# Two attention layers on a 4096-node graph: other sums, accumulators and order in the last microseconds of layer two

## The chip, the cores and the metric

The kernel runs on one core of a Trainium2 chip. The metric is the device time of one execution in microseconds (us); of several runs the median is given. PE is TensorE (matmuls), DVE is VectorE, ACT is ScalarE, POOL is GpSimd, SP is SyncE, which here only issues transfers (DMAs). Line numbers (L1731) are those of the kernel before.

## The reference

The inputs are 4096 rows of 512 features `x`, a sparse 0/1 adjacency matrix `adj`, and the weights of two graph attention layers, all float32. Layer one is a four-headed additive attention with a residual and a layer norm. Layer two, in which the change lies, is masked dot-product attention of eight heads of width 64, then a residual and a layer norm:

```python
adj = jnp.maximum(adjacency_matrix, eye)
q = jnp.einsum('nd,hdk->hnk', node_matrix, Wqs)
k = jnp.einsum('nd,hdk->hnk', node_matrix, Wks)
v = jnp.einsum('nd,hdk->hnk', node_matrix, Wvs)
scores = jnp.einsum('hqk,hmk->hqm', q, k) * kd ** (-0.5)
scores = scores + IDENTITY_BIAS * eye - MASK_VAL * (1.0 - adj)
att = jax.nn.softmax(scores, axis=-1)
return jnp.einsum('hqm,hmk,hko->qo', att, v, Wo)
...
x = _layernorm(x + _L1_gnn_ref(x, adj, L1_gnn_Wks, L1_gnn_Wqs, L1_gnn_Wvs, L1_gnn_Wo), axis=-1)
```

## The kernel before

All engines run their instructions in the order in which the code issues them; there is no scheduler behind it. Layer two works on pairs `(g, m)`: `g` is one of 8 groups of 512 query rows, `m` one of 4 pairs of heads. A pair has 32 units `j`, one for each 128 key rows. For a unit PE computes the scores of two heads into a PSUM tile `s_ps` (128 x 1024, three buffers), ACT takes the exponential in place (L1551), and VectorE multiplies by the mask into a weight tile `p` (L1554). One step later PE multiplies the weights into the output `o_ps` (L1599). A step takes three units; the last pair has its step of two units in the middle (`n_short`), so its last step is of three.

The softmax needs the sum of a pair's weights. `add_up` makes it from the tiles `p`, two at a time: a transfer with addition puts the second of two on the first (L1584, issued from POOL), and POOL adds the result to `q_sum` (L1574). `Later` delays both: `later.at(n, f)` runs `f` at the n-th next `later.step()`, and each step ends in one. POOL also multiplies a pair's output by the reciprocal sums (`on`, L1637), and four small instructions of each layer norm are POOL's (`normal_factors`, L514 to L519).

The last 10 of the last pair's weight tiles are not summed that way: `last_sum` collects them. VectorE adds the first six into one (L1731), and the column sums on PE (`all_sums`, L1605) take six accumulators: `q_sum`, that sum, and the last four tiles themselves.

The output rows are worked in tiles of 128. `project` multiplies a tile of `on` by the output weights, four head pairs `m` accumulating in PSUM (L1663). `close1` adds layer one's row (loaded by `load_y`) on VectorE (L1673), takes the statistics there (L510, L512), the factors on POOL, and one step or more later ACT normalises (L1678) and SP stores. Most tiles are projected and closed while later pairs run. Five are left for the end: tile -5 (of group 6), and the four of group 7, which need the last pair. Behind the last step the code runs: the last products; the VectorE adds; projection and closing of tile -5; the first three quarters of two projections; the column sums; `divide_at_once` (four times a reciprocal, L1655, and a product, L1656, each 128 rows, then two ACT sums, L1659); then, tile by tile, the remaining quarters and the closings, with a test of ranges (`all_in_range`) whose result, `counted` (L1754), decides whether a general path runs instead.

Of the kernel before, what the change touches and what calls it, by code (L numbers as in the profile page):

```python
# [8 lines left out]
F32 = mybir.dt.float32  # L9
# [3 lines left out]
AF = mybir.ActivationFunctionType  # L13
ALU = mybir.AluOpType
# [4 lines left out]
P = 128  # L19
EPS = 1e-5  # L20
# [6 lines left out]
F_MAX = 40.0  # L27
SUM_MIN = 1e-20
SUM_MAX = 1e30
# [400 lines left out]
def tile_gat_then_masked_attention(  # L430
# [16 lines left out]
    nc = tc.nc  # L447
    N, D = x.shape
    H0, D0, _ = weight_u.shape
    H1, _, KD = wks.shape  # L450
    NT = N // P
    G = 512
    NG = N // G
    GT = G // P
    KC = D // P
    HP = P // KD
    NP1 = H1 // HP
# [19 lines left out]
    small = main.enter_context(tc.tile_pool(name="small", bufs=6))  # L477
# [4 lines left out]
    minus_half = const.tile([P, 1], F32, name="minus_half")  # L482
# [36 lines left out]
        nc.gpsimd.tensor_scalar(nb, nb, -1.0, None, op0=ALU.mult)  # L519
        return rs, nb  # L520

    def all_in_range():

        ok = small.tile([P, 8], F32, name="ok")
        ends = small.tile([P, 6], F32, name="ends")
        for n, op in ((0, ALU.max), (2, ALU.min)):
            nc.vector.tensor_reduce(ends[:, 2 + n:4 + n],
                                    span[:, :, n:n + 2].rearrange("p g k -> p k g"), AX.X, op)
        nc.vector.tensor_reduce(ends[:, 0:1], total, AX.X, ALU.add)
        nc.vector.tensor_reduce(ends[:, 1:2], most, AX.X, ALU.add)  # L530
        for n, (value, limit, op) in enumerate((
                (ends[:, 2:3], F_MAX, ALU.is_le), (ends[:, 3:4], F_MAX, ALU.is_le),
                (ends[:, 4:5], -F_MAX, ALU.is_ge), (ends[:, 5:6], -F_MAX, ALU.is_ge),
                (ends[:, 0:1], SUM_MAX, ALU.is_le), (ends[:, 1:2], 1.0 / SUM_MIN, ALU.is_le))):
            nc.vector.tensor_scalar(ok[:, n:n + 1], value, limit, None, op0=op)
        all_ok = small.tile([P, 1], F32, name="all_ok")
        nc.vector.tensor_reduce(all_ok, ok[:, 0:6], AX.X, ALU.min)
        return all_ok
# [6 lines left out]
    counted = const.tile([1, 1], I32, name="counted")  # L545
    right = main.enter_context(ExitStack())
    xp = right.enter_context(tc.tile_pool(name="xp", bufs=2, space=PSUM, side="right"))
    later = Later()
# [18 lines left out]
    with tc.tile_pool(name="l0", bufs=NG) as l0, \  # L567
# [77 lines left out]
        with tc.tile_pool(name="l0s", bufs=2) as sp:  # L645
# [175 lines left out]
            tiles, base = {}, {}  # L821
# [88 lines left out]
            for g in range(NG):  # L910
# [7 lines left out]
                for k, (kind, i) in enumerate(plan):  # L918
                    if k in (0, 3, 7, 10):
                        t = (0, 3, 7, 10).index(k)  # L920
# [63 lines left out]
        with wait_by_tile("l0v", 2) as vp:  # L984
# [91 lines left out]
            for n, (w, h, j) in enumerate(steps):  # L1076
# [7 lines left out]
                p = p_t.pop((w, h, j))  # L1084
                s = sup[w * H0 + h, j // GT][:, j % GT, :]
# [11 lines left out]
    with wait_by_tile("l1", 1) as l1, wait_by_tile("l1a", 2) as lp, \  # L1097
# [417 lines left out]
        with wait_by_tile("l1w", 2) as wp, wait_by_tile("l1o", 1, space=PSUM) as op:  # L1515
# [42 lines left out]
            def add_up(g, m, j):  # L1558

                if j % 2 == 0:
                    return
                a, b = pt.pop((g, m, j - 1)), pt.pop((g, m, j))
                i, n = j // 2, NT // 2
                at_end = (g, m) == pairs[-1]

                def first():
                    q_sum[g, m] = wp.tile([P, HP, G], F32, name="q_sum")
                    nc.gpsimd.tensor_tensor(q_sum[g, m], a, b, op=ALU.add)  # L1570

                def add(p):
                    q = q_sum[g, m]
                    nc.gpsimd.tensor_tensor(q, q, p, op=ALU.add)  # L1574

                if i == 0:
                    later.at(1, first)
                elif at_end and i >= n - 5:
                    last_sum.extend((a, b))
                elif i % 8 == 7:  # L1580
                    later.at(2, lambda: add(a))
                    later.at(3, lambda: add(b))
                else:
                    later.at(2, lambda: nc.gpsimd.dma_start(a, b, accum_op=ALU.add))  # L1584
                    later.at(5, lambda: add(a))

            last_sum = []

            def products(g, m, j):
                if j == 0:  # L1590
# [11 lines left out]
            def all_sums(qs, s):  # L1602
                for n, q in enumerate(qs):
                    for c in range(0, P, MA):
                        nc.tensor.matmul(s[c:c + MA, :], ones[:, 0:MA], q[:, c // KD, :],  # L1605
                                         start=(n == 0), stop=(n == len(qs) - 1))
# [51 lines left out]
                    den = wp.tile([P, G], F32, name="den1", bufs=1)  # L1658
                    nc.scalar.activation(den, src, AF.Copy, accum_out=sums[:, n:n + 1])  # L1659

            def project(g, t, s, ms=range(NP1)):
                for m in ms:
                    nc.tensor.matmul(s, on_t[g][:, m, t * P:(t + 1) * P], wo_sb[:, m, :],  # L1663
                                     start=(m == 0), stop=(m == NP1 - 1))

            def load_y(g, t):
                y_t[g, t] = wp.tile([P, D], F32, name="y1", bufs=5)
                nc.sync.dma_start(y_t[g, t], x1_d[g][t * P:(t + 1) * P, :])

            def close1(g, t, s, wait=4):  # L1670
                i = g * GT + t
                y = y_t.pop((g, t))
                nc.vector.tensor_tensor(y, y, s, op=ALU.add)  # L1673

                rs, nb = normal_factors(y)

                def normalise():
                    nc.scalar.activation(y, y, AF.Identity, bias=nb, scale=rs)  # L1678
                    nc.sync.dma_start(out[i * P:(i + 1) * P, :], y)
                later.at(wait, normalise)  # L1680

            per_pair = [list(range(j, min(j + NB, NT))) for j in range(0, NT, NB)]
            n_short = 5
# [5 lines left out]
            def step(batch, extra_sum, extra_tile, wait=4):  # L1691
                got = [scores(*u) for u in batch]
                if extra_tile and extra_tile not in y_t:
                    load_y(*extra_tile)
                if extra_sum or extra_tile:
                    extra = ps.tile([P, HP, G], F32, name="s_ps")
                if extra_sum:
                    half_sums(q_sum.pop(extra_sum), extra[:, 0, :])
                if extra_tile:
                    project(*extra_tile, extra[:, 1, :])  # L1700
                for u, su in zip(batch, got):
                    weigh(*u, su)
                if extra_tile:
                    close1(*extra_tile, extra[:, 1, :], wait)
                if extra_sum:
                    divide(*extra_sum, extra[:, 0, :])
                for u in batch:
                    add_up(*u)
                for g, m, j in last:
                    products(g, m, j)  # L1710
                for g, m, j in last:
                    if j == NT - 1:
                        o_sb[g, m] = wp.tile([P, G], F32, name="o_sb")
                        o = o_t.pop((g, m))
                        nc.scalar.activation(o_sb[g, m], o[:, 0, :], AF.Copy)
                        nc.vector.tensor_tensor(o_sb[g, m], o_sb[g, m], o[:, 1, :], op=ALU.add)
                last[:] = batch
                later.step()

            for n, (g, m) in enumerate(pairs):  # L1720
                for js in per_pair if n + 1 < len(pairs) else last_pair:
                    whole = len(js) == NB
                    step([(g, m, j) for j in js],
                         None if whole or n < 1 else pairs[n - 1],
                         None if whole or n < NP1 + 1 else tiles[n - NP1 - 1])
            for t in tiles[-5:]:
                load_y(*t)
            step([], None, None)
            later.step()
            for p in last_sum[1:-4]:  # L1730
                nc.vector.tensor_tensor(last_sum[0], last_sum[0], p, op=ALU.add)  # L1731
            step([], None, tiles[-5], 2)
            y_ps = ps.tile([P, HP, G], F32, name="s_ps")
            den_ps = ps.tile([P, HP, G], F32, name="s_ps")
            o_ps = op.tile([P, 2, G], F32, name="o1_ps")
            y_ps = [y_ps[:, 0, :], y_ps[:, 1, :], o_ps[:, 0, :], o_ps[:, 1, :]]
            for n in range(2):
                project(*tiles[n - GT], y_ps[n], range(NP1 - 1))
            all_sums([q_sum.pop(pairs[-1]), last_sum[0]] + last_sum[-4:], den_ps[:, 0, :])
            divide_at_once(*pairs[-1], den_ps[:, 0, :])  # L1740
            for n in range(GT):
                if n + 2 < GT:
                    project(*tiles[n + 2 - GT], y_ps[n + 2], range(NP1 - 1))
                project(*tiles[n - GT], y_ps[n], [NP1 - 1])
                if n == GT - 2:
                    continue
                if n == GT - 1:
                    all_ok = all_in_range()
                    close1(*tiles[n - 1 - GT], y_ps[n - 1], 1)
                close1(*tiles[n - GT], y_ps[n], 1)  # L1750
                later.step()
            count = den_ps[0:1, 1, 0:1]
            nc.tensor.matmul(count, all_ok, ones[:, 0:1], start=True, stop=True)
            nc.vector.tensor_copy(counted, count)  # L1754
            later.flush()


# [34 lines left out]
```

## Time and profile before

| What | Value |
|---|---|
| Median of 4 runs | 3326.25 us (3323.81 to 3326.94) |
| The profiled execution | 3325.09 us, span 3323.2 us |
| PE busy | 3299.7 us (99%) |
| POOL, DVE, ACT busy | 2173.5, 2478.1, 1948.7 us |
| PE's share of the chain that ended last | 92% |
| Last products of layer two | 3283.2 to 3286.0 us |
| VectorE adds of the last weights (L1731) | 3287.36 to 3296.74 us |
| Column sums behind them (L1605) | 3296.78 to 3301.28 us |
| First reciprocal (L1655) | 3301.42 us |
| Last normalised row tile (L1678) | 3315.56 to 3316.37 us |

Times within the span are counted from its start. Busy time is the sum of an engine's instructions; an engine that is busy all the time may still not set the end of a stretch. The chain that ended last is followed back from the last instruction, at each step to what released it. The landing time of a transfer is counted from the start of its issue.

### The profile page before, as it was taken

Reading aid. Unit: us, or ns where it says so; the run is one execution under the profiler, and the core shown is the slowest. Engines: PE = TensorE matmul, PEld = TensorE weight load, DVE = VectorE, ACT = ScalarE, POOL = GpSimd, SP = SyncE. Lnnn points to the kernel's source line nnn. Section 1 sums busy time; section 2 is a strip of 40 time slices with the busy share of each in tenths; the row PEclk is TensorE's granted clock in tenths of the full one; section 3 lists DMA queues with packets and bytes.
Section 4 is the critical chain, followed back from the end, with each engine's and each line's share of the span. In section 5 each row is a group of like instructions: output and inputs, shape, how many; then the busy total and the mean of one; then the engine's idle time right before and its main releaser. Section 6 shows DMA issues by size and latency. Waiting matters only on the chain.

```text
span 3323.2 us, 67217 instructions
## 1 busy us (share of the span) xinstructions
PE 3299.7 (99%) x27160; PEld 1964.4 (59%) x27160; DVE 2478.1 (75%) x3186; ACT 1948.7 (59%) x2439; POOL 2173.5 (65%) x1602
## 2 busy tenths in 40 slices
PE   9999999999999999999999999999999999999998
PEld 8899999999999777733333333333333333333333
DVE  6689899899999677467667666676666766667666
ACT  1367868878776310156656566566665656656564
POOL 5630040040030244389999999999999999999996
PEclk9999999999999999999999999999999999999999
DMA  8989796686532443489898988879888899897984
GB/s 185 228 201 184 219 186 168 151 183 147 137 93 58 110 149 116 167 214 208 190 211 223 227 196 197 209 188 260 199 197 209 188 219 239 194 211 185 213 195 112
DMA packets 398993, 612.06 MB, mean 184 GB/s; under 512 B 167632, under 2 KB 248528, under 8 KB 398672
## 3 DMA queue, kind: packets, MB, share of 16 engines
q0 software_dynamic: 97520, 258.77, 42.7%
q1 hardware_dynamic: 299280, 345.88, 33.6%
q8 instruction: 216, 3.54, 0.4%
q10 hardware_dynamic: 1872, 3.02, 0.4%
q14 instruction: 105, 0.86, 0.1%
HBM read 315.87 MB, written 109.25 MB: 128 GB/s over the span
## 4 chain that ended last, share of the span: by engine, by line
PE 92%; POOL 3%; DMA 2%; DVE 1%; issue 1%; ACT 0%; POOLq 0%; SPq 0%; DVEq 0%; ACTq 0%
PE o_ps L1087 27%; PE o_ps L1599 24%; PE s_ps L1138 24%; PE o_ps L846 4%; PE s_ps L1663 3%; PE s_ps L1298 2%; PE s_ps L1248 2%; PE s_ps L1255 2%; DMA p<-p 2%; POOL q_sum L1574 2%; PE x_ps L1255 1%; PE x_ps L1248 1%; POOL p L1584 1%; PE s_ps L1618 0%; DMA y_sb<-in_x_dram 0%
## 5 line engine op out<-in xcount | busy, mean ns | idle before, releaser
L1574 POOL TENSOR_TENSOR q_sum<-q_sum,p 128x1024 f32<-128x1024 f32 x538 | 1375.2, 2556 | 66.4 <-DMA p<-p 44.0
L1554 DVE TENSOR_TENSOR p<-s_ps,adjT 128x1024 f32<-128x1024 f32 x896 | 1044.3, 1216 | 469.2 <-ACT s_ps L1551 435.3
L1551 ACT ACTIVATE s_ps<-s_ps 128x1024 f32<-128x1024 f32 x1021 | 967.6, 1006 | 597.0 <-PE s_ps L1138 596.6
L1138 PE MATMUL s_ps<-q_sb,k_sb 64*64 64x512 f32 x8192 | 943.9, 589 | 2.1 <-DVE p L1554 2.0
L1599 PE MATMUL o_ps<-p,v_sb 64*64 64x512 f32 x8192 | 943.6, 590 | 0.0
L1087 PE MATMUL o_ps<-sup_t,p 128*128 128x129 f32 x8192 | 915.7, 275 | 1.2 <-DVE p L640 1.2
L1087 PEld LDWEIGHTS o_ps<-sup_t,p 128*128 128x128 f32 x8192 | 915.3, 192 | 1.7 <-DVE p L640 1.4
L640 DVE SCALAR_TENSOR_TENSOR p<-fr_t,dj,az 128x1024 f32<-128x1024 f32 x512 | 650.2, 1284 | 66.1 <-PE o_ps L1087 37.9
L1138 PEld LDWEIGHTS s_ps<-q_sb,k_sb 64*64 64x64 f32 x8192 | 312.1, 133 | 569.9 <-issue 451.5
L1599 PEld LDWEIGHTS o_ps<-p,v_sb 64*64 64x64 f32 x8192 | 310.2, 133 | 570.6 <-issue 560.4
L624 ACT ACTIVATE z<-fr_t,f 128x1024 fp8e4<-128x1024 f32 x512 | 557.3, 1143 | 102.0 <-DVE az L635 101.7
L1584 POOL DMA_DIRECT2D p<-p x412 | 439.0, 1305 | 10.1 <-PE o_ps L1599 9.2
L1063 POOL DMA_DIRECT2D agg<-base_d x32 | 29.1, 1217 | 386.8 <-DMA sup_t<-sup_d 204.7
L585 POOL COPY seen<-token 128x1 f32<-128x1 f32 x24 | 10.9, 455 | 356.8 <-DVE token L583 356.8
L1554 DVE TENSOR_TENSOR p<-s_ps,md 128x1024 f32<-128x1024 f32 x128 | 150.8, 1218 | 66.8 <-ACT s_ps L1551 59.6
L635 DVE TENSOR_TENSOR az<-adjT,z 128x512 int32<-128x512 int32 x256 | 175.3, 685 | 2.9 <-ACT z L624 1.7
L600 ACT ACTIVATE adjT<-stage 128x1024 fp8e4<-128x1024 bf16 x128 | 130.9, 1051 | 16.6 <-DMA stage<-adj_d 16.6
L1663 PE MATMUL s_ps<-wo_sb,on 128*128 128x512 f32 x240 | 110.8, 604 | 0.0
L1633 ACT ACTIVATE r<-r_h 32x256 f32<-32x256 f32 x248 | 102.3, 412 | 2.9
L1049 ACT ACTIVATE agg<-o_ps,rinv 128x128 f32<-128x128 f32 x128 | 42.1, 370 | 70.5 <-DVE den L1042 46.8
L1322 ACT ACTIVATE v<-s_ps 128x256 f32<-128x256 f32 x28 | 10.7, 383 | 115.0 <-PE s_ps L1298 99.9
L1663 PEld LDWEIGHTS s_ps<-wo_sb,on 128*128 128x128 f32 x240 | 43.3, 189 | 55.9 <-issue 55.7
(275 smaller groups left out, 2231.6 us busy)
## 6 DMA issues: line engine op xcount, KB each, us to landing
p<-p POOLq DMA_DIRECT2D x412, 512.0 KB, 9.1
k_sb<-k_d SPq DMA_DIRECT2D x128, 512.0 KB
v_sb<-v_d SPq DMA_DIRECT2D x128, 512.0 KB
adj_d<-in_adj_dram POOLq DMA_DIRECT2D x32, 1024.0 KB, 11.1
sup_t<-sup_d SPq DMA_DIRECT2D x120, 258.0 KB
fr_t<-fr_d SPq DMA_DIRECT2D x16, 1024.0 KB
adjT_d<-adjT SPq DMA_DIRECT2D x32, 512.0 KB
adjT<-adjT_d SPq DMA_DIRECT2D x32, 512.0 KB
```

Of the source, the lines that this page charges most:

```text
L624: nc.scalar.activation(z[:, k, :], fr_t[w, h][:, 0, :], AF.Sign, bias=fs[j // GT][:, 0, (j + k) % GT, h:h + 1], saturate=False)
L635: nc.vector.tensor_tensor(az.bitcast(I32), adjT[w, j // CJ][:, j % CJ:j % CJ + 2, :].bitcast(I32), z.bitcast(I32), op=ALU.bitwise_and)
L640: nc.vector.scalar_tensor_tensor(p, fr[:, 1, :], dj[j // GT][:, j % GT, h:h + 1], az_t[w, h, j // 2][:, j % 2, :], op0=ALU.max, op1=ALU.mult)
L846: nc.tensor.matmul(out[:, t * HD:(t + 1) * HD], xb[:, c, t * P:(t + 1) * P], wb[:, c, :], start=not more and t == 0 and c == 0, stop=c == ...
L1087: nc.tensor.matmul(o[t // BK][:, t % BK, :], p[:, t * P:(t + 1) * P], s, start=(j == 0 and t % BK == 0), stop=(j == NT - 1), skip_group_ch ...
L1138: nc.tensor.matmul(s[c:c + MS, e, :], k[r, a + c:a + c + MS], qt[g, m][r, :], start=True, stop=True)
L1551: nc.scalar.activation(s, s, AF.Exp, scale=float(KD) ** -0.5)
L1554: nc.vector.tensor_tensor(p, s, keep[:, None, :].to_broadcast([P, HP, G]), op=ALU.mult)
L1574: nc.gpsimd.tensor_tensor(q, q, p, op=ALU.add)
L1584: later.at(2, lambda: nc.gpsimd.dma_start(a, b, accum_op=ALU.add))
L1599: nc.tensor.matmul(o[c, n, :], v[r, j % CH, c], p[r, e, :], start=(j == 0), stop=(j == NT - 1))
L1663: nc.tensor.matmul(s, on_t[g][:, m, t * P:(t + 1) * P], wo_sb[:, m, :], start=(m == 0), stop=(m == NP1 - 1))
```

## The change

The change touches the end of layer two alone, in six places.

1. In `add_up`, weights 22 to 27 of the last pair are now added in twos by transfers, and only one tile of each two is kept; weights 28 to 31 are kept as before. `last_sum` is 22, 24, 26, 28, 29, 30, 31.
2. VectorE adds all seven into tile 22, in two parts (`gather`): 24, 28 and 29 ahead of the addition of the last pair's two output halves, then 30, 31 and 26. The column sums take two accumulators: `q_sum` and tile 22.
3. Tile -5 is projected ahead of the last products instead of behind them; its closing comes behind all of VectorE's adds.
4. ACT copies layer one's rows into the four PSUM accumulators of the last four tiles, and the projections add onto them (`onto`); the rows are loaded earlier in the program.
5. The partial projections and the last products are issued as part 0, part 1, column sums, part 2, rest 0, rest 1, part 3, rest 2, rest 3, and the closings behind all of them.
6. The closings (`close_in_place`) take statistics and normalisation from PSUM. Three are normalised by ACT as before; the last one on VectorE, with two small POOL instructions instead of four. The range test is split: what doesn't need the sums comes ahead of the column sums.

```diff
                 elif at_end and i >= n - 5:
-                    last_sum.extend((a, b))
+                    later.at(2, lambda: nc.gpsimd.dma_start(a, b, accum_op=ALU.add))
+                    last_sum.append(a)
...
-            def project(g, t, s, ms=range(NP1)):
+            def project(g, t, s, ms=range(NP1), onto=False):
                 for m in ms:
                     nc.tensor.matmul(s, on_t[g][:, m, t * P:(t + 1) * P], wo_sb[:, m, :],
-                                     start=(m == 0), stop=(m == NP1 - 1))
+                                     start=(m == 0 and not onto), stop=(m == NP1 - 1),
+                                     skip_group_check=onto)
...
+            def close_in_place(g, t, s, vector=False, meanwhile=None):
+                i = g * GT + t
+                y = y_t.pop((g, t))
+                st = small.tile([P, 6], F32, name="bn_st")
+                nc.vector.bn_stats(st, s)
+                mv = small.tile([P, 2], F32, name="bn_mv")
+                nc.vector.bn_aggr(mv, st)
+                rs = small.tile([P, 1], F32, name="bn_rs")
+                nc.gpsimd.tensor_scalar(rs, mv[:, 1:2], EPS, None, op0=ALU.add)
+                nc.gpsimd.tensor_tensor(rs, rs, minus_half, op=ALU.pow)
+                if vector:
+                    meanwhile()
+                    nc.vector.tensor_scalar(y, s, mv[:, 0:1], rs, op0=ALU.subtract,
+                                            op1=ALU.mult)
+                else:
+                    nb = small.tile([P, 1], F32, name="bn_nb")
+                    nc.gpsimd.tensor_tensor(nb, mv[:, 0:1], rs, op=ALU.mult)
+                    nc.gpsimd.tensor_scalar(nb, nb, -1.0, None, op0=ALU.mult)
+                    nc.scalar.activation(y, s, AF.Identity, bias=nb, scale=rs)
+                nc.sync.dma_start(out[i * P:(i + 1) * P, :], y)
...
+            extra = ps.tile([P, HP, G], F32, name="s_ps")
+            project(*tiles[-5], extra[:, 1, :])
+            y_ps = ps.tile([P, HP, G], F32, name="s_ps")
+            y_ps = [y_ps[:, 0, :], y_ps[:, 1, :]]
+            for n in range(2):
+                nc.scalar.activation(y_ps[n], y_t[tiles[n - GT]], AF.Copy)
+            a22, a24, a26, *others = last_sum
+            gather(a22, a24, *others[:2])
+            all_products()
             later.step()
-            for p in last_sum[1:-4]:
-                nc.vector.tensor_tensor(last_sum[0], last_sum[0], p, op=ALU.add)
-            step([], None, tiles[-5], 2)
-            y_ps = ps.tile([P, HP, G], F32, name="s_ps")
+            gather(a22, *others[2:], a26)
+            for _ in range(5):
+                later.step()
+            close1(*tiles[-5], extra[:, 1, :], 1)
             den_ps = ps.tile([P, HP, G], F32, name="s_ps")
             o_ps = op.tile([P, 2, G], F32, name="o1_ps")
-            y_ps = [y_ps[:, 0, :], y_ps[:, 1, :], o_ps[:, 0, :], o_ps[:, 1, :]]
-            for n in range(2):
-                project(*tiles[n - GT], y_ps[n], range(NP1 - 1))
-            all_sums([q_sum.pop(pairs[-1]), last_sum[0]] + last_sum[-4:], den_ps[:, 0, :])
+            more_ps = ps.tile([P, HP, G], F32, name="s_ps")
+            y_ps += [o_ps[:, 0, :], more_ps[:, 0, :]]
+            for n in range(2, GT):
+                nc.scalar.activation(y_ps[n], y_t[tiles[n - GT]], AF.Copy)
+            later.step()
+            known = in_range_so_far()
...
+            part(0)
+            part(1)
+            all_sums([q_sum.pop(pairs[-1]), a22], den_ps[:, 0, :])
             divide_at_once(*pairs[-1], den_ps[:, 0, :])
...
+            part(2)
+            rest(0)
+            rest(1)
+            part(3)
+            rest(2)
+            rest(3)
+            close_in_place(*tiles[-GT], y_ps[0])
+            close_in_place(*tiles[1 - GT], y_ps[1])
+            all_ok = all_in_range(known)
+            close_in_place(*tiles[2 - GT], y_ps[2])
             count = den_ps[0:1, 1, 0:1]
             nc.tensor.matmul(count, all_ok, ones[:, 0:1], start=True, stop=True)
-            nc.vector.tensor_copy(counted, count)
+            close_in_place(*tiles[3 - GT], y_ps[3], True, lambda: nc.vector.tensor_copy(
+                counted, count))
```

`part(n)` is the first three quarters of a projection and `rest(n)` its last quarter; `gather(into, *others)` adds the others to `into`, one VectorE instruction each; `all_products` is the part of `step` that issues the products of the step before.

## The prediction

> **What bounds the kernel now.** I read the page first, then the chain of work that ended last from 3180 us on, then each engine's timeline over the last 50 us, then the landing times of the last accumulating transfers. On the page PE is busy 3299.7 us of the 3323.2 us span and PE makes 92% of the chain: two long matmul stages, which the diff does not touch. Every edit lies behind the last scores, so only the stretch from about 3278 us to the end can move. The chain there:
>
> ```profile
> 3280.82 5.19 PE o_ps L1599 x48
> ...
> 3286.67 0.69 DVE o_sb L1716
> 3287.36 2.32 DVE p L1731
> 3289.68 0.02 issue
> 3289.70 3.26 DVE p L1731
> 3292.96 0.02 issue
> 3292.99 1.24 DVE p L1731
> ...
> 3296.78 4.50 PE s_ps L1605 x40
> 3301.28 2.77 PE o_ps L1663 x6
> ...
> 3313.08 0.71 DVE bn_st L510
> ...
> 3315.56 0.81 ACT y L1678
> ```
>
> Columns are start, duration, what. The end is serial: the last products, five VectorE adds (3287.36 to 3296.74), the column sums of six accumulators on PE (q_sum before, then 40 rows in 4.50 us), then division and closings with VectorE the busiest, and ACT's last output at 3316.37. The remaining 6.83 us to 3323.2 are the last store and the program's end. Two of the five adds take 2.32 and 3.26 us instead of 1.24; they lie beside POOL's adds, in POOL's timeline:
>
> ```profile
> 3276.77 1.76 POOL L1584 DMA_DIRECT2D p<-p  x2
> 3277.94 2.98 POOL L1574 TENSOR_TENSOR q_sum<-q_sum,p 128x1024 f32<-128x1024 f32 x1
> 3280.24 1.52 POOL L1584 DMA_DIRECT2D p<-p  x1
> 3280.87 2.20 POOL L1637 TENSOR_TENSOR on<-o_sb,r 128x512 f32<-128x512 f32 x1
> 3282.20 3.18 POOL L1574 TENSOR_TENSOR q_sum<-q_sum,p 128x1024 f32<-128x1024 f32 x1
> 3286.23 5.63 POOL L1574 TENSOR_TENSOR q_sum<-q_sum,p 128x1024 f32<-128x1024 f32 x2 [0.85 <-DMA p<-p]
> ```
>
> The reader is to see that POOL never rests until 3283 and once waits for a transfer, and that the last transfer of before (weights 20 and 21) is issued only at 3280.24: POOL runs its list late.
>
> **The change, part by part.**
>
> *The pair sums by transfer.* Weights 22+23 and 24+25 become transfers, due one step before the "on" product of L1637; 26+27 becomes one that is due behind the q_sum adds of 16 and 18. In POOL's list the first two therefore follow the issue at 3280.24. Successive issues start 0.6 us apart (3276.77 and 3277.37 in POOL's timeline) and take about 0.9 us each, so they begin at about 3280.8 and 3281.4. When do they land? The landing answers for the two transfers issued at 3277.4 and 3280.24 are
>
> ```profile
> DMA to landing us min/median/max: 8.7/8.7/8.7
> DMA to landing us min/median/max: 8.3/8.3/8.3
> ```
>
> hence 3286.1 and 3288.5: 2.45 us apart, although they were issued 2.9 us apart. The DMA share is 1.01 from 3276.8 to 3286.5, so they queue for the engines. Two more behind them land at 3288.5 + 2 x 2.45: 3291.0 and 3293.4; I take 3293.5 for the second. Bounds: alone, a transfer in this stretch landed 5.2 us after issue, giving 3286.6 at the early end; the first two of the burst at 3249 landed 3.4 us apart, giving 3295.3 at the late end. I take the spacing of the very transfers they follow.
>
> *VectorE's sums.* The first add of the new list needs both transfers, and everything behind it on VectorE queues: five more adds, the addition of the two output halves (L1716) and the closing of tile -5. With POOL's last add over by then (its list grows by three issues, about 2.7 us, and loses the slowing by VectorE, so it ends at about 3292.8), an add takes the undisturbed 1.24 + 0.02 us. Three adds from 3293.5 reach 3297.3, L1716 (0.7) 3298.0, three more 3301.8. The third transfer, issued near 3289.5, is queued behind the second and lands at about 3296, before its add at 3300.5: no cost. So **the summed weights are ready at 3301.8 instead of 3296.74: 5.1 us later.** The products come behind the early projection of tile -5 (3.63 us), end near 3289.5, and are hidden by this wait.
>
> *The column sums.* Four accumulators fewer, 32 rows of 40: what waits for the VectorE sum shrinks from 4.50 to 0.9 us. The q_sum part, like the first two partial projections (2.6 us each), is over by about 3295.6, inside the wait.
>
> *What is queued between.* Before, the closing of tile -5 on VectorE (0.70 + 0.71 + 0.18, 1.6 with gaps) ran beside the column sums. Now it follows the adds: 3303.4. The first half of the range test (two reductions and four of six comparisons, 0.5 from L527 and L535) ends at 3303.9. PE has been ready since 3302.7, so VectorE sets the start: **the first reciprocal at 3303.9 instead of 3301.42, 2.5 us late.**
>
> *Rows copied into four accumulators.* Four ACT copies of 0.6 us (L1715's row, same size). Two run near 3283, where ACT rests; the others wait for L1716 and for tile -5's addition, until 3302.5, and are over by 3303.1, ahead of the partial products that need them: no cost. In return four VectorE additions of 0.69 (L1673) go, and the statistics read PSUM; no row shows that, so I bound it by the 0.69 of L1673 (which reads PSUM) and L510 (SBUF): equal.
>
> *The closings.* Four reciprocals with their products take 3301.42 to 3306.20, 4.8 us: now done at 3308.7. PE, at full clock, ends the paired last products at about 3311.7. Statistics for tile 0: 0.85 to 3309.6. Then POOL is late next: four small instructions per closing take 3312.55 to 3314.00, 1.5 us with the gap, three closings in a row 3309.6 to 3314.1. The last closing has two instead of four (L514, L516: 0.88), to 3315.0, and ends in a VectorE normalisation instead of ACT's, 0.7 by L1673: 3315.8 with gaps. From first reciprocal to last output: 11.9 us, against 3301.42 to 3316.37, 14.95. **Gain here 3.05.**
>
> *Loads.* Four row loads move ahead of two steps in program order, but on SP they stand behind the same store as before (issued 3272.58) and were issued right after it, at 3272.97, already. No change; if SP held them longer, they would still be 10 us early.
>
> *Sum at full clock:* 2.5 later, 3.05 shorter: -0.55 us.
>
> **The clock.** PE now rests from 3295.6 to 3301.8, 6.2 us. What a rest does shows at the very end of before, in the windows (the last three figures are clock, DMA share, GB/s):
>
> ```profile
> 3313.00:3313.20 0.20, 0.00 (x0) 0.00 (x0) 0.17 (x2) 0.00 (x0) 0.20 (x1) 1.00 0.00 0
> 3313.20:3313.40 0.20, 0.00 (x0) 0.00 (x0) 0.20 (x1) 0.00 (x0) 0.20 (x1) 0.50 0.60 236
> ```
>
> The last projection ended at 3310.06; 3.1 us later (a 0.19 us count between) the granted clock is half. A rest of 3.3 us early in the span (11.1 to 14.4) kept 1.00, so a few us decide; 6.2 us is twice that. No row shows a recovery under work. Ends: at once, -0.55; or not before the end: sums 1.8, partials 5.2 each, last products 1.75 each, last product at 3321.0, output at 3323.6, +7.2. I take the falling edge as the nearest row: 3.1 us at half clock from 3301.8 to 3304.9. The sums end at 3303.6, still before VectorE is free; the third partial at 3306.9; the last product at 3312.9 instead of 3311.7. Tile 2's statistics end at 3313.0, POOL's third closing at 3314.5, its last at 3315.4, the output at 3316.2: -0.2 in all.
>
> [...]
>
> **Own time.** The profiled execution took 3325.09 us (span 3323.2 and 1.9 around it); the median of the runs is 3326.25, 1.16 above. -0.2 gives 3324.9 for such an execution and 3326.1 for a median.
>
> **Rivals.**
> 1. *The transfers land early and the wait is short.* For it: the DMA engines have nothing else after 3286.5. Against it: the measured spacing. At the early bound PE's own work (partials and sums to about 3296.5) and VectorE's (recip at 3297.1) decide: 4.3 earlier than before, and 3.05 shorter: -7.3, 3319.0. Halfway, about -3: 3323.
> 2. *The half clock lasts.* The slow side, one mechanism: PE's granted clock from 3301.8 on. It decides once half clock costs PE over about 1.3 us, when the last product comes after POOL's queue would have been ready for it. Price up to +7.2 over before: 3333.5; a recovery after 6 us costs about +1, 3327.3.
> 3. *The transfers land later:* 3.4 us apart, the second at 3295.3, puts 1.8 on everything behind it: 3328.
> 4. *The change moves nothing:* the new accumulators replace exactly what they hide. It has the same time as the forecast and cannot be told from it by time, only by the chain.
>
> **How the numbers follow.** Forecast (with rival 4) 0.50, own range 3324.5 to 3327.7 with the runs' spread of 3 us; rival 1 0.25; rival 2 0.15; rival 3 0.10. A difference of 0.2%, 6.65 us, is about what a measurement of this kernel tells from no change. Only the ends of rivals 1 and 2 pass it: faster 0.03, slower 0.06, the rest 0.91. The range leaves out those ends and a little of each rival: 3321.5 to 3330.
>
> **What would show it.** In the trace of after: the first VectorE sum starting at a transfer's landing near 3293.5 (right), or near 3287 (rival 1); six adds of 1.24 each, none of 2 to 3; eight sum rows behind them; VectorE, not PE, ahead of the first reciprocal; POOL's small instructions back to back in the closings; the granted clock at half somewhere from 3299 to 3306, or at 1.00 throughout (then -0.55). I am wrong if the chain runs through PE at half clock to the end, or if the first reciprocal starts before 3300.

## The result

The changed kernel takes 3329.91 us (median of 32 runs, 3326.22 to 3333.45), the kernel before 3326.08 us (52 runs, 3323.37 to 3329.37). The ratio is 1.0012, with a 95% interval from 1.0007 to 1.0017: 3.8 us slower, where the forecast had 0.2 us faster. The time lies inside the range and inside the 0.2% that I called no change, but the direction is wrong, and the interval does not hold 1.

The profiled execution of after took 3331.2 us (span 3329.4), that of before 3325.09 us (3323.2). These 6.2 us are not all the change's. The last step's scores start at 3278.07 us in before and 3280.51 us in after; the code ahead of them is the same in both, so 2.4 us are a difference between two executions; after is already 2.97 us behind at 29 us (the last section says how). From here on, times are counted from the start of those scores ("anchored"). From there to the end of the span before takes 45.14 us and after 48.90: 3.76 us more, close to the 3.83 between the medians.

| Anchored, us | before | forecast | after |
|---|---|---|---|
| Second of the new transfers landed | (none) | 15.4 | 14.85 |
| Weights summed on VectorE | 18.66 | 23.7 | 22.87 |
| First reciprocal | 23.35 | 25.8 | 27.26 |
| From there to the last output | 14.95 | 12.3 | 13.83 |
| From there to the end of the span | 6.84 | 6.8 | 7.81 |

The difference is 3.9 later at the first reciprocal, 1.1 gained in the closings, 1.0 lost behind the last output: 3.8 in all.

### The profile page after: what moved, and what is told of

The parts are those of the page before. It is cut to its first block, busy times and chain, and to the rows that moved or that the text cites. A ratio compares the mean times of both kernels' runs of the same rounds, so it can differ in the third digit from the quotient of the medians.

```text
span 3329.4 us, 67162 instructions
## 1 busy us (share of the span) xinstructions
PE 3301.3 (99%) x27128; PEld 1966.0 (59%) x27128; DVE 2475.2 (74%) x3184; ACT 1949.5 (59%) x2442; POOL 2173.1 (65%) x1603
## 4 chain that ended last, share of the span: by engine, by line
PE 91%; POOL 4%; DMA 3%; issue 1%; DVE 1%; ACT 0%; POOLq 0%; SPq 0%; DVEq 0%
PE o_ps L1093 27%; PE o_ps L1612 24%; PE s_ps L1144 24%; PE o_ps L852 4%; PE s_ps L1676 3%; DMA p<-p 2%; PE s_ps L1304 2%; POOL q_sum L1580 2%; PE s_ps L1254 2%; PE s_ps L1261 2%; PE x_ps L1261 1%; PE x_ps L1254 1%; POOL p L1593 1%; PE s_ps L1631 0%; PE s_ps L1300 0%
```

## The profile after

The chain of waits of after (start, duration, what), in the same stretch as that of before:

```profile
3283.83 11.53 DMA p<-p
...
3295.38 1.24 DVE p L1600
...
3303.29 0.69 DVE y L1687
3303.99 0.14 issue
3304.12 3.55 PE s_ps L1618 x16
...
3307.77 0.97 DVE r L1668
...
3315.02 0.79 ACT y L1714
3315.81 0.02 issue
3315.83 0.71 DVE bn_st L1700
...
3320.79 0.81 DVE y L1708
```

The forecast is there in part: a transfer's landing starts the first sum (L1600), and small steps of VectorE and POOL follow the reciprocals. Two links are not in it. The sums on PE (L1618, now 16 rows) start at the end of tile -5's addition (L1687), and statistics on VectorE (L1700) start at the end of an ACT normalisation (L1714). The same two stand in after's waits of PE and of VectorE (who <- for what: us, times, longest):

```profile
PE s_ps L1618 <- DVE y L1687: 6.6, 1, 6.6
```

```profile
DVE p L1600 <- DMA p<-p: 9.2, 1, 9.2
DVE r L1668 <- PE s_ps L1618: 2.4, 1, 2.4
DVE bn_st L1700 <- ACT y L1714: 2.4, 1, 2.4
```

Neither is a wait for data. The sums of `q_sum` don't use tile -5, and tile 1's statistics don't use tile 0's output. What they share is a PSUM tile: `den_ps` takes the buffer of `extra`, which holds tile -5's projection until L1687 has read it; and the accumulators of tiles 0 and 1 are two halves of one `y_ps`. (The program as built gives `den_ps` and `extra` the same PSUM address, and `more_ps`, which is asked for later, the third buffer, free since the last scores.) That this is what makes the waits is for the experiments to show.

After's windows show the clock (behind the duration PE, PEld, DVE, ACT, POOL busy, then the granted clock, DMA share, GB/s):

```profile
3297.40:3300.40 3.00, 0.15 (x1) 0.00 (x0) 2.97 (x4) 0.64 (x2) 0.00 (x0) 1.00 0.00 0
3300.40:3300.60 0.20, 0.00 (x0) 0.00 (x0) 0.20 (x1) 0.20 (x1) 0.00 (x0) 0.85 0.00 0
3300.60:3304.10 3.50, 0.00 (x0) 0.01 (x1) 3.40 (x5) 0.28 (x1) 0.00 (x0) 0.50 0.00 0
3304.10:3307.20 3.10, 3.08 (x16) 0.67 (x16) 1.22 (x8) 0.69 (x1) 1.21 (x4) 0.50 0.00 0
3307.20:3307.40 0.20, 0.20 (x4) 0.00 (x0) 0.00 (x0) 0.12 (x1) 0.00 (x0) 0.58 0.00 0
3307.40:3307.60 0.20, 0.20 (x5) 0.04 (x1) 0.00 (x0) 0.00 (x0) 0.00 (x0) 1.00 0.00 0
```

PE stops at 3297.55, the clock halves at 3300.5, PE starts again at 3304.12 and has full speed from 3307.4. The 16 rows of sums run at half clock, but for the last 0.3 us.

## The experiments

All are in this table (anchored; "closings" is first reciprocal to last output, "end" last output to end of span). The ratio is against the kernel before on the same chip.

| Run | First reciprocal | Closings | End | End of span | Ratio, 95% |
|---|---|---|---|---|---|
| before | 23.35 | 14.95 | 6.84 | 45.14 | |
| after | 27.26 | 13.83 | 7.81 | 48.90 | 1.0012 [1.0007, 1.0017] |
| e1_own_buffer | 25.62 | 14.85 | 6.66 | 47.13 | 1.0007 [0.9998, 1.0016] |
| e2_tiles_apart | 27.28 | 15.36 | 7.90 | 50.54 | 1.0016 [1.0007, 1.0025] |
| e3_sums_undone | 27.18 | 13.83 | 7.95 | 48.97 | 1.0012 [1.0003, 1.0021] |
| e4_close_in_wait | 26.17 | 14.19 | 7.63 | 47.99 | 1.0010 [1.0001, 1.0019] |
| e5_stats_first | 27.38 | 12.07 | 7.21 | 46.66 | 1.0006 [0.9997, 1.0015] |
| e6_kept_busy | 24.75 | 13.85 | 7.91 | 46.51 | 1.0004 [0.9995, 1.0013] |
| e7_all_mended | 21.88 | 14.63 | 8.15 | 44.66 | 0.9998 [0.9989, 1.0007] |
| e8_transfers_kept | 26.16 | 13.86 | 8.83 | 48.85 | 1.0009 [1.0000, 1.0018] |
| e9_last_by_scalar | 28.07 | 14.77 | 7.33 | 50.17 | 1.0008 [0.9999, 1.0017] |
| e10_adds_ahead | 19.89 | 14.63 | 7.76 | 42.29 | 0.9996 [0.9987, 1.0005] |
| e11_both | 19.89 | 15.18 | 6.65 | 41.72 | 0.9991 [0.9982, 1.0000] |
| e12_part_early | 22.47 | 14.48 | 7.45 | 44.40 | 0.9997 [0.9988, 1.0006] |

A single execution carries chance: the second transfer lands at 14.82 to 14.91 in some and at 15.41 to 15.54 in e1, e8 and e9, and "end" varies by 1 us and more. I therefore judge by the link that an edit was to move, and by the medians last.

### e1: the sums' buffer

```diff
-            den_ps = ps.tile([P, HP, G], F32, name="s_ps")
...
+            part(0)
+            part(1)
+            den_ps = ps.tile([P, HP, G], F32, name="s_ps")
+            q = q_sum.pop(pairs[-1])
+            all_sums([q], den_ps[:, 0, :], final=False)
             gather(a22, *others[2:], a26)
...
-            part(0)
-            part(1)
-            all_sums([q_sum.pop(pairs[-1]), a22], den_ps[:, 0, :])
+            all_sums([a22], den_ps[:, 0, :], first=False)
```

> The changed kernel, with the partial projections 0 and 1 and the column sums of q_sum issued ahead of tile -5's closing, so that the sums get a PSUM buffer of their own and no longer the one that tile -5's projection holds. Counted from the start of the last step's scores, the changed kernel has its first reciprocal at 27.3 us, before has it at 23.35. Theory A (the sums wait for tile -5's buffer, and then run all 16 rows at half clock behind the VectorE sums): q_sum's rows run in the wait, only eight rows stay behind it, first reciprocal at 24.9, bounded by VectorE's range test, 2.4 us earlier; time about 3327.5. Theory B (the wait for the transfers is the whole price): the first reciprocal moves under 1 us, time 3329 to 3330.

PE's timeline of e1 (start, busy, line, operation, last the idle time before it and its releaser):

```profile
3298.56 1.07 PE L1618 MATMUL s_ps<-q_sum,ones 128*32 128x512 f32 x8
3305.13 1.94 PE L1618 MATMUL s_ps<-p,ones 128*32 128x512 f32 x8 [5.51 <-DVE p L1600]
3307.00 4.21 PE L1677 MATMUL o_ps<-wo_sb,on 128*128 128x512 f32 x6
```

`q_sum`'s rows now run right behind the partials, in 1.07 us at full clock, and the rest waits for the weights alone. The first reciprocal comes 1.64 earlier, although the transfer landed 0.62 later: 2.26, near the expected gain. So the buffer made that wait. But 1.02 of it is given back: the third partial projection takes 4.21 us at half clock, 2.84 in after, and tile 0's statistics wait 0.9 for PE. In after, the 16 late rows had taken up most of the half clock, which ended at 3307.4; here it lasts to 3309.8 and reaches the projections.

### e2: the accumulators apart

Tiles 0 and 2 share a buffer, tiles 1 and 3 have their own.

```diff
-            y_ps += [o_ps[:, 0, :], more_ps[:, 0, :]]
-            for n in range(2, GT):
+            y_ps = [y_ps[0], o_ps[:, 0, :], y_ps[1], more_ps[:, 0, :]]
+            for n in (1, 3):
```

> The changed kernel, with tiles 0 and 2 instead of 0 and 1 in the two halves of one PSUM buffer (part 2 issued where part 1 was, and the other way round), so that successive closings read different buffers. Theory A (tile 1's statistics wait until ACT has read tile 0, because both lie in one buffer): the gap of 2.4 us before tile 1's statistics falls to what the last product leaves, POOL's four closings stand back to back, last output 1.8 us earlier counted from the first reciprocal (13.8 to about 12.0); time about 3328. Theory B: that gap is not what ends the closings; no change, 3329 to 3330.

The waits of VectorE in e2:

```profile
DVE bn_st L1700 <- PE s_ps L1676: 3.0, 1, 3.0
...
DVE bn_st L1700 <- ACT y L1714: 1.0, 1, 1.0
```

It is slower, by my own design: the first of these is tile 0's statistics, which wait for the last product of tile 2, in the other half of its buffer; the second is tile 2's, which wait for tile 0's normalisation. It supports that waits go by whole tile and in program order. Tile 1, whose accumulator now lies in another buffer than tile 0's, has its statistics 0.84 us behind tile 0's, where after had 3.28: that wait is gone, as theory A had it, but the new ones cost more (closings 15.36).

### e3: the sums undone

Weights 22 to 27 as in before: no late transfers, five VectorE adds, 48 rows of sums.

```diff
-                    later.at(2, lambda: nc.gpsimd.dma_start(a, b, accum_op=ALU.add))
-                    last_sum.append(a)
+                    last_sum.extend((a, b))
...
-            all_sums([q_sum.pop(pairs[-1]), a22], den_ps[:, 0, :])
+            all_sums([q_sum.pop(pairs[-1]), last_sum[0]] + last_sum[-4:], den_ps[:, 0, :])
```

> The changed kernel with its sums undone: weights 22 to 31 kept apart as before, five VectorE adds, six accumulators for the column sums; projections and closings as changed. Theory A: the weights are ready about 3.5 to 4.5 us earlier, PE never rests long, but all 48 rows of column sums stand behind tile -5's addition, so that the first reciprocal comes about 26 us after the last step's scores began, 1 to 2 us earlier than changed; time 3328 to 3329. Theory B (the wait for the transfers is the whole price): first reciprocal at about 23.4 as before, and with the changed closings 3 to 4 us faster than changed, 3325 to 3327.

The weights are ready at 19.25 instead of 22.87, and yet the first reciprocal comes at 27.18. PE's timeline of e3 says why:

```profile
3297.18 1.06 PE L1615 MATMUL s_ps<-q_sum,ones 128*32 128x512 f32 x8 [2.96 <-DVE y L1684]
3298.03 6.20 PE L1615 MATMUL s_ps<-p,ones 128*32 128x512 f32 x40
```

All 48 rows now stand behind tile -5's addition (L1684 here), and 3.4 us of that at half clock: 40 rows in 6.20 us where before needed 4.50. So the weights' 3.6 us are lost as long as the rows stand behind tile -5's addition: there are three times as many of them here, and the clock is at half for part of them. The price of the late transfers and that of the shared buffer don't simply add.

### e4: tile -5 closed in the wait

```diff
+            close1(*tiles[-5], extra[:, 1, :], 1)
+            known = in_range_so_far()
             a22, a24, a26, *others = last_sum
             gather(a22, a24, *others[:2])
```

(and no longer behind the adds)

> The changed kernel, with tile -5's closing and the first half of the range test moved ahead of the VectorE sums, into VectorE's 9 us wait for the transfers. Theory A: tile -5's buffer comes free early, q_sum's rows run in the wait, and 2.1 us of VectorE work leave the path; eight rows behind the sums, at half clock 1.8 us: first reciprocal at 24.7 us after the last step's scores began, at full clock 23.8 (changed 27.3); time 3326.5 to 3327.5. Theory B: the sums are ready when they were and the time stays within 1 us of the changed kernel's.

`q_sum`'s rows start at 16.97, as in e1, this time with the shared buffer merely freed earlier. The first reciprocal gains 1.1 and not 2.5: the first three adds take 4.94 us instead of 3.74, and the eight rows behind them take 1.94 at half clock. VectorE's and POOL's timelines of e4 show what lies beside the adds:

```profile
3294.14 4.94 DVE L1600 TENSOR_TENSOR p<-p,p 128x1024 f32<-128x1024 f32 x3 [3.78 <-DMA p<-p]
```

```profile
3293.13 2.35 POOL L1580 TENSOR_TENSOR q_sum<-q_sum,p 128x1024 f32<-128x1024 f32 x1
```

POOL's last addition to `q_sum` comes late, behind tile -5's small POOL instructions, and runs into the first add; in after it is over at 14.72, before the adds start.

### e5: statistics of tiles 0 and 1 first

```diff
-            close_in_place(*tiles[-GT], y_ps[0])
-            close_in_place(*tiles[1 - GT], y_ps[1])
+            mvs = [stats(y_ps[n]) for n in range(2)]
+            close_in_place(*tiles[-GT], y_ps[0], mv=mvs[0])
+            close_in_place(*tiles[1 - GT], y_ps[1], mv=mvs[1])
```

> The changed kernel, with the statistics of tiles 0 and 1 both taken before tile 0 is normalised, so that no statistics have to wait for ACT's reading of the same PSUM buffer. From first reciprocal to last output the changed kernel takes 13.8 us. Theory A (tile 1's statistics wait for ACT's reading of tile 0): the wait of 2.4 us in front of them goes, POOL's closings stand back to back, 12.0 us, 1.8 us less; time about 3328. Theory B (the closings are bound by something else, such as the last product): 13.8 us or little less, 3329.5 to 3330.

VectorE's timeline of e5:

```profile
3312.47 0.69 DVE L1698 BATCH_NORM_STATS2 bn_st<-s_ps 128x6 f32<-128x512 f32 x1
3313.19 0.18 DVE L1700 BATCH_NORM_AGGREGATE bn_mv<-bn_st 128x2 f32<-128x6 f32 x1
3313.29 0.67 DVE L1698 BATCH_NORM_STATS2 bn_st<-s_ps 128x6 f32<-128x512 f32 x1
```

The second statistics start 0.82 behind the first, where after had 3.28. The closings take 12.07 us, and nothing else was touched: the wait was worth 1.76 us, and it came from the order in the program.

### e6: PE kept busy

As e1, with `q_sum`'s rows issued six times in a row; only the last time counts, the other 40 rows are extra work.

```diff
+            for _ in range(5):
+                all_sums([q], den_ps[:, 0, :])
             all_sums([q], den_ps[:, 0, :], final=False)
```

> The run with a buffer of its own for the sums (first reciprocal at 25.6 us after the last step's scores began, 14.85 us from there to the last output), with q_sum's eight rows issued six times over, each time anew, to keep PE busy in the wait for the VectorE sums. Only the clock and 40 added rows differ. Theory A (the half clock costs in the sums and in the third partial projection): granted clock 1.00 throughout, the last eight rows take 0.9 us instead of 1.9 and the third partial 2.8 instead of 4.2; first reciprocal unchanged at 25.6, because VectorE's range test sets it, and 13.8 to the last output, 1.0 us less. Theory B (the clock does not matter): no change.

PE's timeline of e6, against that of e1:

```profile
3294.82 5.36 PE L1618 MATMUL s_ps<-q_sum,ones 128*32 128x512 f32 x48
3300.76 1.06 PE L1618 MATMUL s_ps<-p,ones 128*32 128x512 f32 x8 [0.58 <-DVE p L1600]
3301.76 2.84 PE L1677 MATMUL o_ps<-wo_sb,on 128*128 128x512 f32 x6
```

The rest is 0.58 us instead of 5.51, the clock is 1.00 in all of e6's windows from 3300 to 3310 (0.50 in e1's from 3304 to 3308), the eight rows take 1.06 instead of 1.94 and the third partial 2.84 instead of 4.21. The last output comes 1.87 us earlier than in e1 (0.6 of it may be the earlier landing). With 40 useless rows this kernel cannot be told from the kernel before, while after is 3.8 us behind that.

### e7 and e8: all of it mended, without and with the late transfers

e7 has e3's sums, tile -5 closed in the wait, `q_sum`'s and the last four weight tiles' rows early, only one partial projection ahead of them instead of two, and e5's order; the diff is against e3, without e5's part and without the move of the projections. e8 is e4 with e5's order.

```diff
+            close1(*tiles[-5], extra[:, 1, :], 1)
+            known = in_range_so_far()
...
             all_products()
+            part(0)
+            den_ps = ps.tile([P, HP, G], F32, name="s_ps")
             later.step()
-            gather(last_sum[0], *last_sum[1:-4])
+            all_sums([q_sum.pop(pairs[-1])] + last_sum[-4:], den_ps[:, 0, :], final=False)
+            gather(last_sum[0], *last_sum[1:-4])
...
+            all_sums([last_sum[0]], den_ps[:, 0, :], first=False)
```

> The changed kernel's rows in the accumulators and its closings, with the sums of the kernel before (weights 22 to 31 kept apart, five VectorE adds, six accumulators), tile -5 closed while VectorE would wait, the rows of the five accumulators that are ready early issued beside VectorE's adds into a buffer of their own, one partial projection ahead of them and three behind, statistics of tiles 0 and 1 first. Theory A: weights ready at about 19.3 us after the last step's scores began, first reciprocal at 20.3 (before 23.35, changed 27.3), then PE-bound, last output at 34 to 35 (before 38.3, changed 41.1); time 3321.5 to 3323, faster than both. Theory B (PSUM accumulators with layer one's rows and closings from PSUM are slower in themselves): last output not before 38, 3326 or more.

> The changed kernel with its transfers and sums, tile -5 closed in VectorE's wait and the statistics of tiles 0 and 1 first. Beside the run with everything mended it shows what the wait for the transfers costs. Theory A: first reciprocal at 26.2 us after the last step's scores began, as in the run with the closing in the wait alone, 12.4 us from there to the last output; last output at 38.6, time 3326.5 to 3328, so about 4 us of the remaining difference to the mended sums is the wait for the transfers with its half clock. Theory B: the closings gain nothing, 3329.4.

e7 ends 4.2 us (anchored) before after, and e8 as after does. Between them lie the late transfers: 4.28 us at the first reciprocal, half clock included (e8's third partial takes 4.64 us). Not all of it is the wait as after has it: e8's weights are ready at 24.04 and not at 22.87, because its transfer landed 0.56 later and its first three adds took 4.36 us. e7 missed my 20.3 by 1.6: its adds waited 1.3 us for the output addition in front of them, and then took 7.62 us beside POOL's late addition.

### e9 to e12: the last closing, and a better order

e9 is after, and e11 is e10, with the last tile normalised on ACT. e10 is e7 with two moves (second diff); e12 is e11 with the second partial early.

```diff
-            close_in_place(*tiles[3 - GT], y_ps[3], True, lambda: nc.vector.tensor_copy(
-                counted, count))
+            close_in_place(*tiles[3 - GT], y_ps[3])
+            nc.vector.tensor_copy(counted, count)
```

```diff
+            later.step()
             close1(*tiles[-5], extra[:, 1, :], 1)
             known = in_range_so_far()
...
+            gather(last_sum[0], *last_sum[1:-4])
             all_products()
             part(0)
             den_ps = ps.tile([P, HP, G], F32, name="s_ps")
-            later.step()
             all_sums([q_sum.pop(pairs[-1])] + last_sum[-4:], den_ps[:, 0, :], final=False)
-            gather(last_sum[0], *last_sum[1:-4])
```

> The changed kernel, with the last tile normalised by ScalarE like the other three (four small GpSimd instructions instead of two) and the count of the range test copied behind it. Theory A (the last two stores crowd each other: in the changed kernel their issues start 0.97 us apart, in the kernel before 1.53, and the end came 7.81 us after the last output instead of 6.84): the last output comes about 0.5 later, the last two issues are again about 1.5 apart, and the stretch from the last output to the end of the span is 6.8 to 7.0; the end of the span, counted from the start of the last scores, stays or is up to 0.5 us earlier. Theory B (the length of the last stretch has nothing to do with what normalises the last tile: its eight values so far lie between 6.7 and 8.8): it stays at 7.5 to 8, and the end comes about 0.5 us later.

> As e7 (sums as in the kernel before, tile -5 closed in the wait, q_sum's rows and the first partial projection early, statistics of tiles 0 and 1 first), with two moves: VectorE's five adds go ahead of the addition of the two output halves, which waits for the last products, and GpSimd's last addition to q_sum goes ahead of tile -5's four small instructions. Theory A (in e7 the first reciprocal was late because VectorE waited 1.32 us for the products' output in front of the adds, and because GpSimd's late addition slowed them to 7.62 us instead of 6.3): weights ready about 18.0 us after the start of the last scores instead of 20.62, first reciprocal at 19.3 instead of 21.88, last output at 34, end of the span near 42 instead of 44.66; time about 3322, some 3 us under the kernel before. Theory B (rows on TensorE bound it, 40 of them at half clock): first reciprocal not before 21, time as e7.

> As e10, with the last tile normalised by ScalarE as in e9. If the stretch behind the last output follows the last two stores' distance (theory A of e9): last output 0.5 later than in e10, the end equal or 0.5 earlier. If not (theory B): the end 0.5 later. Times differ by less than the runs' spread; the traces decide.

> As e11, with the second tile's partial projection (three matmuls, 1.3 us) moved from behind the last eight column sums to behind the first tile's, ahead of q_sum's rows, where TensorE waits 1.3 us for GpSimd's last addition. Theory A (in e11 the closings of tiles 2 and 3 wait 3.37 us for TensorE, which is the late one behind the reciprocals): first reciprocal unchanged at 19.9 us after the start of the last scores, last output 1.3 earlier, about 33.8, end of the span at 40.4 with 6.65 behind the last output; time some 4.5 to 5 us under the kernel before. Theory B (VectorE's reciprocals and GpSimd's small instructions bound the closings, not TensorE): the last output stays at 35.

**The end.** Where VectorE normalises the last tile, the last two stores are issued closer together (0.97 us apart in after, 1.53 in before) and the last issue on SP is longer; here after's and then e8's (SP's timeline of each):

```profile
3321.62 0.60 SPq L1715 DMA_DIRECT2D out_dram<-y  x1
```

```profile
3318.76 1.33 SPq L1719 DMA_DIRECT2D out_dram<-y  x1
```

It takes 0.60 us in after and 1.33 in e8, and 0.33 in before, where ACT ends. In e5 and e10 SP's rows end 0.9 us behind the last output, in e9 and e11, where ACT ends, 0.3 to 0.4. That much is shown. The whole stretch behind the last output is 6.66 to 8.83 us in the ten kernels that end on VectorE (mean 7.78) and 6.65 to 7.45 in before, e9, e11 and e12 (mean 7.07): 0.7 us on average, against an output that comes 0.55 earlier (e10 to e11). Single values overlap, and e9's 7.33 fits neither theory. Nor is e9 a clean pair with after: its last output came 1.75 us later than after's and not 0.5, as its transfer landed 0.69 later and its half clock lasted 10.24 us. So the VectorE ending gains nothing that I can show, and whether it costs stays open.

**The order.** e10's first reciprocal is at 19.89, 2.0 before e7's and 3.5 before before's; it missed 19.3 because PE, not VectorE, is last there. Its median, 3324.56 us, is only 1.06 under the kernel before, where some 3 were expected and its trace has 2.9. e11's median is 3322.37 us, 3.25 under the kernel before on the same chip, with 1.0000 just at the edge of the interval. It has no late transfer, no shared wait and no rest of PE. PE's timeline of e11:

```profile
3289.40 2.84 PE L1674 MATMUL s_ps<-wo_sb,on 128*128 128x512 f32 x6
3292.17 1.06 PE L1615 MATMUL s_ps<-q_sum,ones 128*32 128x512 f32 x8
3293.06 4.48 PE L1615 MATMUL s_ps<-p,ones 128*32 128x512 f32 x40
```

e12 rests on a misreading of these rows. I took the partial for 1.3 us and saw a gap of 1.3 behind it; it is 2.8 (six matmuls), and there is no gap. So 2.8 us of work went in front of a PE that was already the last: the first reciprocal comes 2.58 later, the last output 1.88.

## Why the prediction was wrong

**Right.** The two late transfers follow the spacing of those ahead of them (2.47 us); the second landed 0.6 earlier than forecast, and rivals 1 and 3 are out. The six adds are undisturbed. VectorE's timeline of after:

```profile
3295.38 3.74 DVE L1600 TENSOR_TENSOR p<-p,p 128x1024 f32<-128x1024 f32 x3 [9.17 <-DMA p<-p]
...
3299.64 3.74 DVE L1600 TENSOR_TENSOR p<-p,p 128x1024 f32<-128x1024 f32 x3
```

The weights are ready 4.2 us later than in before (forecast 5.1). The half clock came and went within 6.8 us, with 3.25 us of it under work; I had taken 3.1. Rival 2's mechanism was there, but it did not last: by itself it is not the 3.8 us. No run shows the recovery after 6 us that rival 2 prices: from the new start of work to full speed it was 3.2 (e2, after) to 5.5 us (e8).

Two readings in the prediction were off. In the rows shown, POOL's first rest begins at 3285.4 and not at 3283, which moved nothing: POOL's last addition to `q_sum` ended where the sum had it, at 14.7. And the early rest of 3.3 us that kept the clock at 1.00 does not show that the length of a rest decides: after rests 3.26 us there, and its clock fell to 0.50 (last section).

**Failed: "The q_sum part, like the first two partial projections (2.6 us each), is over by about 3295.6, inside the wait."** The partials were. `q_sum`'s rows waited 6.57 us for tile -5's addition, and ran behind everything else at half clock: 3.55 us for 16 rows, where I had put eight rows in front of the first reciprocal. VectorE was ready at 24.85, 1.0 ahead of the forecast, and then waited 2.41 us for PE. e1 and e4 moved those rows to 16.97 in two different ways. The half clock has its part in the wait: e6's 48 rows in 5.36 us give, as an estimate, 1.8 us for 16 rows at full clock, and the wait would then have been about 0.6. I asked which data an instruction needs, and not which buffer its output takes and who reads that last. This term is 2.4 - 1.0 = +1.4 against the forecast.

**Failed: "three closings in a row 3309.6 to 3314.1".** POOL's small instructions are back to back only for tiles 1 to 3. Tile 1's statistics waited 2.38 us for tile 0's normalisation. e5 took 1.76 us away with the order alone. Against the forecast (12.3) this term is +1.5.

**Failed: the 6.83 us behind the last output, taken over from before.** It was 7.81 in this execution, +1.0. The longer last issue on SP is seen; what makes the rest of it, and whether the VectorE ending does, stays open. The last closing's own row, 0.81 on VectorE instead of the 0.7 I took, is inside the second term.

1.4 + 1.5 + 1.0 = 3.9, from -0.17 to 3.76. Both prices of the waits are of the order of the spread of runs; the traces show them, the times alone would not.

**The transfers.** My own sum said that they cost 2.5 us at the first reciprocal and that the closings win it back. The closings could (12.07 in e5; the forecast had 12.3 with the half clock). But e8 against e7 puts the price of the transfers at up to 4.3, against an order in which the old sums run early.

## What to carry to other kernels

For every instruction that is moved ahead of a wait, look up which buffer its output takes and who reads that buffer last in program order; in these programs, accesses to two halves of one tile waited for each other across engines as if they were one (2.38 us in after, 3.0 and 1.0 in e2). In e1, a rest of 5.51 us in front of TensorE had two prices, its length and the half clock behind it, and the second fell on what ran next: eight rows took 1.94 us and a partial projection 4.21, against 1.06 and 2.84 in e6, behind a rest of 0.58. In a serial end, take each engine's queue in program order to its last instruction, the stores too, ahead of adding up gains.

## What the runs showed of the hardware

From windows of 0.2 us, the half clock at the column sums lasted 3.41 us in e3, 6.83 in after, e1, e2, e4, e5 and e8 (6.82 to 6.83), and 10.24 in e9: in these eight traces one, two and three times 3.41. The edges of e9, in its windows (granted clock third from the end), and then those of e3:

```profile
3296.60:3296.80 0.20, 0.00 (x0) 0.00 (x0) 0.20 (x2) 0.00 (x0) 0.00 (x0) 0.73 0.00 0
3306.80:3307.00 0.20, 0.20 (x1) 0.00 (x0) 0.20 (x2) 0.00 (x0) 0.00 (x0) 0.67 0.00 0
```

```profile
3298.20:3298.40 0.20, 0.20 (x7) 0.00 (x0) 0.20 (x4) 0.00 (x0) 0.12 (x2) 0.51 0.00 0
3301.60:3301.80 0.20, 0.20 (x4) 0.00 (x0) 0.00 (x0) 0.00 (x0) 0.00 (x0) 0.96 0.92 358
```

In e3 the clock fell at 3298.2, 1.0 us after PE had started again: its rest of 2.96 us was paid for when it was already over. From the stop of work to the fall it was 2.2 (e9) to 4.8 us (e8), from the new start of work to full speed 3.2 (e2, after) to 5.5 (e8). Neither stands at one distance from what PE did; what sets them is not shown. The price of a rest depended on it: in e1 full speed came at 3309.8, 2.8 us into the third partial (4.21 us), in after at 3307.4, just ahead of it (2.84).

Nearly the same rest cost nothing in one execution and 2.9 us in another. Some 11 us into before and after PE rests for 3.3 us. PE's timeline behind that rest, first of before, then of after (the rest in brackets):

```profile
14.39 1.99 PE L846 MATMUL o_ps<-w_sb,xT 128*128 128x256 f32 x8 [3.32 <-ACT z L863]
```

```profile
14.49 3.78 PE L852 MATMUL o_ps<-w_sb,xT 128*128 128x256 f32 x8 [3.26 <-ACT z L869]
```

In before the granted clock stayed at 1.00, in after it was 0.50 from 14 to 20 us. After was 0.10 us behind at the start of these rows and 2.97 behind from there on (the row that starts at 23.13 in before starts at 26.10), in code that the change does not touch. The longer of the two rests kept the clock and the shorter did not: the length of such a rest alone does not decide here.
